# Keeping column-tiled matmul runs together, and moving score maxima ahead on VectorE, in a two-layer macaron transformer kernel

## The chip, the cores and the metric

The kernel runs on one core of one Trainium2 chip. The metric is the device time of one execution in microseconds (us), as a median of several runs. All intermediate results stay on the chip or in its HBM; there is one launch.

The engines are named as in the profile: PE is TensorE (PEld are its weight loads), DVE is VectorE, ACT is ScalarE, POOL is GpSimd, SP is the queue that issues most DMAs. Each engine works through its own list of instructions in the order that was fixed when the kernel was built, and waits on semaphores for what the others make.

## The reference, cut to what matters

The input is 16 sequences of 512 tokens of 128 features. Two layers are applied:

```
x = x + 0.5*ffn0(ln(x)); x = x + attn0(ln(x)); x = x + 0.5*ffn0(ln(x))     # layer 0
x = x + 0.5*ffn1(ln(x)); x = x + attn1(ln(x)); x = x + 0.5*ffn1(ln(x))     # layer 1
```

`ffn0` is a gated feed-forward net whose inputs and weights are rounded to a block-wise 4-bit format. `attn1` is a causal linear attention, and `ffn1` an attention over the batch, followed by a mixture of experts. The change is mostly about `attn0`, attention with clipped relative positions, 16 heads of 8 features:

```
score = einsum('bhqd,bhkd->bhqk', q, k) + einsum('bhqd,qkd->bhqk', q, pe_k)
attn  = softmax(score, axis=-1)
ctx   = einsum('bhqk,bhkd->bhqd', attn, v) + einsum('bhqk,qkd->bhqd', attn, pe_v)
```

Here `pe_k[q,k]` and `pe_v[q,k]` are rows of a table of 129 positions, picked by the distance `k-q` clipped to -64..64.

## The kernel before, in words

The kernel is written as Python generators that emit instructions. `interleave` decides in which order the generators advance, and so the program order. The framework then schedules: it plays the program forward on a model of the engines and, whenever an engine is free in that model, issues on it the ready instruction of the lowest priority number. By default that number is the place in program order. Two tools bend this. `tc.issue_after(ins)` forbids that the instructions of a block are issued before `ins` on the same engine. `tc.high_priority()` gives the instructions of a block a number ahead of everything of ordinary priority. What comes out is a fixed order for each engine; on the chip nothing is reordered by priority any more.

**Layer 0** works in 32 units, one for each sequence `b` and half of its queries (256 of 512). For each unit there are these streams:

- `Attn0.maxima` makes 32 score tiles of 128 keys by 512 (32 queries times 16 heads) in PSUM. A tile is made by `scores`: four matmuls with the keys (L263), and eight more with the position table (L267) if the tile lies in the band where the distance is not clipped. VectorE reduces each tile to its maxima (L341), and at the end of the unit the row maxima are written through DMA into the query operand `BD`, so that the second pass subtracts them.
- `Attn0.main` makes the same 32 tiles again. ScalarE takes the exponential of each into `PT` (L369), one of four SBUF tiles of 128 keys. After each eight tiles (`kt`, a block of 128 keys), a run of 16 matmuls multiplies `PT` with the values into two PSUM banks, `av`. Then, for each half `hb` of the unit whose last in-band key block this was, two runs multiply `PT` with the clipped position table `TV` into one PSUM bank, `rps`. ScalarE copies `rps` out (L404), it makes a trip through HBM, and `Attn0.fin` adds it to the rest (L423) and applies the output projection.
- `FFN.half` is the feed-forward net for half a sequence: transposes, matmuls of 352 columns, and a chain of rounding steps on VectorE and GpSimd. It runs once ahead (`head`) and once behind (`tail`) the attention.
- `Attn0.prep` and `prepV` make queries, keys and values for a sequence two ahead.

The score tiles of both passes share one PSUM pool of three banks (`pS`, the tile name is `sps`). A further two banks serve all the rest (`mps`).

The runs on `av` and `rps` are **column-tiled**: each matmul has only 32 output rows and uses a quarter of the array's columns (`tile_position=(0,cg*32)`), and four neighbours in the list, one for each quarter, work side by side. `Attn0.run` emits such a run: its first matmul (L272) at ordinary priority, the others (L274) behind it by `issue_after`. An `rps` run takes a pair of query blocks `bb`; for each it goes through the in-band key blocks `k` in rising order, with eight matmuls each. Over layer 0 there are 128 `av` runs of 16 matmuls and 128 `rps` runs of 28 matmuls on average. Each float32 matmul stands in the trace as two records, so such runs have 32 and on average 56 records.

**Layer 1** uses `Attn1.burst` (L853, L855) in the same way for its column-tiled runs: with the running state (`a_su`), with the masked products (`a_at`) and for the state's update (`a_kt`).

Of the kernel before, what the change touches and what calls it, by code (L numbers as in the profile page):

```python
# [13 lines left out]
ALU = mybir.AluOpType  # L14
AX = mybir.AxisListType
# [130 lines left out]
class Attn0:  # L146
# [123 lines left out]
    def run(a, mms):  # L270

        r=a.nc.tensor.matmul(*mms[0][0],**mms[0][1])  # L272
        with a.s.tc.issue_after(getattr(r,"ins",r)):
            for p,q in mms[1:]: a.nc.tensor.matmul(*p,**q)  # L274
    def prep(a, b, xb, wk, pM):
        s=a.s; nc=a.nc
# [55 lines left out]
    def maxima(a, b, half, wk, pS, pM):  # L332

        nc=a.nc; i=b%2
        u=(2*b+half)%3; BD=a.BD[u]; TQ=a.TQ[u]; KS=a.KS[b%2]; MD=a.MD[half]
        mx=wk.tile([128,4,16,8],F32,name="mx")
        for bb in range(8):
            for kt in range(4):
                ps=pS.tile([128,512],F32,name="sps")
                a.scores(ps,kt,half,bb,BD,TQ,KS)  # L340
                r=nc.vector.tensor_reduce(mx[:,kt,:,bb],ps.rearrange("p (i c) -> p i c",c=32),axis=AX.X,op=ALU.max,apply_transpose=True)  # L341
                a.last=r.ins if hasattr(r,"ins") else r
                yield
        a.last=None
        mk=wk.tile([128,2,8,8],F32,name="mk")
        for hh in range(2):
            nc.vector.tensor_reduce(mk[:,hh],mx.rearrange("p k (x s) b -> p s b x k",s=2)[:,hh],axis=AX.X,op=ALU.max)
        ps=pS.tile([128,512],F32,name="sps")
        nc.tensor.transpose(ps[:,:128],mk.rearrange("p s b x -> p (s b x)"),a.ident)
        mt=wk.tile([128,32],F32,name="mt"); mn=wk.tile([128,32],F16,name="mn")  # L350
        nc.vector.tensor_reduce(mt,ps[:,:128].rearrange("p (c q) -> p q c",c=4),axis=AX.X,op=ALU.max)
        nc.vector.tensor_scalar(mn,mt,-1.0,None,ALU.mult)
        for hh in range(2): nc.sync.dma_start(MD[hh*8:hh*8+8].rearrange("h (y j) -> y h j",j=4),mn[hh*64:hh*64+64].rearrange("p (h j) -> p h j",j=4))
        for j in range(4):
            nc.sync.dma_start(BD[28+32*j:29+32*j,:,j,:],MD.rearrange("(g j) q -> j g q",j=4)[j:j+1])
        yield

    def main(a, b, half, X, wk, big, pS, pA, pM):
        s=a.s; nc=a.nc; i=b%2
        u=(2*b+half)%3; BD=a.BD[u]; TQ=a.TQ[u]; KS=a.KS[b%2]; V=a.V[b%2]; RD=a.RD[half]; cr=a.cr[0]  # L360
        av=[pA.tile([128,512],F32,name=f"av{z}") for z in range(2)]
        RV=wk.tile([128,4,4,4,16],F32,name="RV")
        PT=[None]*4
        for kt in range(4):
            pt=big.tile([128,16,256],F32,name="PT"); PT[kt]=pt
            for bb in range(8):
                ps=pS.tile([128,512],F32,name="sps")
                a.scores(ps,kt,half,bb,BD,TQ,KS)
                nc.scalar.activation(pt[:,:,bb*32:bb*32+32].rearrange("p h (x j) -> p x h j",j=4),ps.rearrange("p (x h j) -> p x h j",x=8,j=4),AF.Exp)  # L369
                yield  # L370
            vs=a.vers(kt,half)
            mms=[]
            for z in range(4):
                for cg in range(4):
                    h=z*4+cg
                    o=av[z//2][cg*32:cg*32+32,(z%2)*256:(z%2)*256+256]
                    fs=(kt==0 and z%2==0)
                    mms.append(((o,V[:,2*kt-1+vs,h*9:h*9+32],pt[:,h,:]),dict(start=fs,stop=(kt==3),skip_group_check=True,tile_position=(0,cg*32))))
            a.run(mms)
            for _ in range(4): yield  # L380
            for hb in range(2):
                bl=range(hb*4,hb*4+4)
                ks=[k for k in range(4) if any(a.inband(k,half*8+x) for x in bl)]
                if max(ks)!=kt: continue
                rps=pA.tile([128,512],F32,name="rps")
                first=[True]*4
                mms=[]
                for bb in bl:
                    blk=half*8+bb
                    kk=[k for k in ks if a.inband(k,blk)]  # L390
                    for k in kk:
                        for x in range(8):
                            cg=x%4; col=(bb-hb*4)*128+(x//4)*64
                            v0=(blk*32-k*128+a.UO)//8
                            mms.append(((rps[cg*32:cg*32+32,col:col+64],a.TV[a.vers(k,half)][:,x,v0-8*a.vers(k,half):v0-8*a.vers(k,half)+4,:].rearrange("p v d -> p (v d)"),
                                PT[k][:,:,bb*32+4*x:bb*32+4*x+4]),
                                dict(start=first[cg],stop=(k==kk[-1]),skip_group_check=True,tile_position=(0,cg*32))))
                            first[cg]=False
                    if bb%2:
                        a.run(mms); mms=[]  # L400
                        yield
                        yield
                for c in range(4):
                    nc.scalar.copy(RV[:,:,c,:,hb*8:hb*8+8].rearrange("p j z a -> p a z j"),rps.rearrange("p (a z c j) -> p c a z j",a=8,z=4,j=4)[:,c])  # L404
                yield

        nc.sync.dma_start(RD[:,:4*8*1024].rearrange("x (r f) -> x r f",f=1024),RV)
        for c in range(4):
            src=bass.AP(tensor=RD.tensor,offset=RD.offset+c*64,ap=[[1024,8],[8*1024+256,16],[1,64]])
            nc.sync.dma_start(cr[c*32:c*32+8].rearrange("p (xj f) -> p xj f",f=64),src)  # L410
        cx=wk.tile([128,4,256],F32,name="cx")
        for zz in range(2):
            nc.scalar.copy(cx[:,2*zz:2*zz+2,:].rearrange("p z (b j x) -> p (z b) x j",j=4,x=8),av[zz].rearrange("p (y x j) -> p y x j",x=8,j=4))
        a.pend[b,half]=cx,cr
        yield
# [42 lines left out]
def layer0(tc, s, w, src, dst, nb=16):  # L458
# [3 lines left out]
    with ExitStack() as c:  # L462
# [44 lines left out]
        with tc.tile_pool(name="wp",bufs=1) as wp:  # L507
            for b in range(3): xload(b)
            F=FFN(s,w["L0_ffn_w_gate"],w["L0_ffn_w_up"],w["L0_ffn_w_down"],wp,pF)
            ffn2=lambda f,b: interleave((f(b,0),21,0,.8),(f(b,1),21,.2,1))  # L510
            ffn2(head,0)
            A=Attn0(s,wp,pS,*[w[P+n] for n in names])
            def run(g):
                for _ in g: pass
            run(prep(0)); run(prepV(0)); loads(0); run(mxs(0,0))
            FFN1.pre(s,wp,[pA.tile([128,512],F32,name=f"av{z}") for z in range(2)]+[pA.tile([128,512],F32,name="rps")],w)
        big=c.enter_context(tc.tile_pool(name="big",bufs=3))
        loads(1); ffn2(head,1); run(prep(1)); run(part(14)); ffn2(head,2)
        S=[(part(99999),33*2*nb,W['part'],2*nb+W['part'])]
        for b in range(nb):  # L520
# [262 lines left out]
class Attn1:  # L783
# [67 lines left out]
    def burst(a, mms):  # L851

        r=a.nc.tensor.matmul(*mms[0][0],**mms[0][1])  # L853
        with a.s.tc.issue_after(getattr(r,"ins",r)):
            for p,q in mms[1:]: a.nc.tensor.matmul(*p,**q)  # L855
    def main(a, t, bq, wk, pM, pP, pA):

# [181 lines left out]
```

## Time and profile before

| what | us |
|---|---|
| runs of the kernel | 3673.34, 3679.3, 3679.36 |
| median | 3679.3 |
| the profiled execution, its own time | 3669.38 |
| its span (first to last instruction) | 3667.4 |
| start-up: weights, first unit | 0 to about 180 of the span |
| layer 0 in steady work | about 180 to 2020 |
| layer 1: first `ffn1` | about 2020 to 2570 |
| layer 1: attention with parts of `ffn1` | about 2570 to 3420 |
| layer 1: end | about 3420 to 3668 |

The profile is one execution. Its own time is 2 us over the span, and 10 us under the median of the runs. Busy times of PE count matmuls that overlap only once, but a matmul counts as busy until its modelled end. To see what a matmul costs the ones behind it, this document takes the distance from its start to the start of the next. The mean granted clock of TensorE was 0.90 of full speed over the span.

### The profile page before, as it was taken

The numbers are of one execution on the slowest core, as the hardware profiler recorded it, in microseconds if no ns is written. First come the engines' busy times: TensorE is split into PE (matmuls) and PEld (weight loads), VectorE is DVE, ScalarE is ACT, GpSimd is POOL, SyncE is SP. The second block draws the span as 40 slices with busy tenths as digits, with TensorE's granted clock in tenths as the row PEclk, the third lists the DMA queues.
The fourth block names the chain that finished last, engine by engine and source line by source line (L and its number), as shares of the span: only waits on it lengthen the run. The fifth ranks groups of instructions, "written<-read, shape, count | busy, mean of one in ns | idle before, by whom it ended". The sixth has DMA issues, their size and how long they took to land. (4 is left out here: it accounts for less than half of the span.)

```text
span 3667.4 us, 95252 instructions
## 1 busy us (share of the span) xinstructions
PE 2895.4 (79%) x40077; PEld 2076.7 (57%) x40077; DVE 2453.7 (67%) x6508; ACT 1702.8 (46%) x3391; POOL 839.6 (23%) x789
## 2 busy tenths in 40 slices
PE   5579888898988989899988278882688888878570
PEld 3357666777767776677776144441465555555340
DVE  5568678777877788777764457774546656545357
ACT  3145445544554545545545155542455455445242
POOL 4122122222222222222101222222112121111226
PEclk8789999999999999999999588885899999999785
DMA  3232122322232122322210101104322222121301
GB/s 109 52 86 70 46 63 59 78 64 47 55 78 71 45 63 64 77 63 45 68 38 20 40 24 35 38 30 110 90 73 58 59 65 67 36 61 36 123 19 46
DMA packets 290159, 217.23 MB, mean 59 GB/s; under 512 B 77402, under 2 KB 257476, under 8 KB 289604
## 3 DMA queue, kind: packets, MB, share of 16 engines
q1 hardware_dynamic: 284468, 207.72, 21.5%
q8 instruction: 315, 5.16, 0.6%
q10 hardware_dynamic: 5264, 3.43, 0.4%
q14 instruction: 112, 0.92, 0.1%
HBM read 110.28 MB, written 100.78 MB: 58 GB/s over the span
## 5 line engine op out<-in xcount | busy, mean ns | idle before, releaser
L341 DVE TRANSPOSE_TENSOR_REDUCE mx<-sps 128x16 f32<-128x512 f32 x1024 | 706.0, 701 | 262.3 <-PE sps L267 138.6
L263 PE MATMUL sps<-a_BD,a_KS 128*128 128x128 f16 x8192 | 745.5, 222 | 156.2 <-DVE mx L341 96.2
L369 ACT ACTIVATE PT<-sps 128x512 f32<-128x512 f32 x1024 | 580.4, 598 | 554.0 <-PE sps L267 289.1
L263 PEld LDWEIGHTS <-a_KS 128*128 128x128 f16 x8192 | 540.3, 98 | 309.2 <-issue 257.7
L59 POOL TENSOR_TENSOR ln_rs<-ln_ve,negh 128x4 f32<-128x4 f32 (+1 forms) x192 | 175.3, 921 | 857.1 <-DVE ln_ve L58 778.3
L267 PE MATMUL sps<-a_TQ,a_ET 128*128 128x64 f16 x7168 | 370.2, 194 | 0.3 <-issue 0.3
L722 DVE SCALAR_TENSOR_TENSOR moe<-mps,oh,moe 128x128 f32<-128x128 f32 x896 | 289.8, 341 | 112.7 <-PE mps L720 99.7
L79 POOL TENSOR_TENSOR q_M<-q_y,q_M 128x704 f32<-128x704 f32 (+2 forms) x129 | 159.2, 1235 | 862.4 <-DVE q_y L78 650.7
L720 PE MATMUL mps<-f_W,T 128*128 128x512 f32 x512 | 302.9, 714 | 17.9 <-DVE moe L722 13.6
L267 PEld LDWEIGHTS <-a_ET 128*128 128x128 f16 x7168 | 309.8, 99 | 6.9 <-issue 6.5
L274 PE MATMUL av<-PT,a_V 128*32 128x256 f32 x3840 | 251.4, 386 | 0.0
L895 DVE TENSOR_TENSOR a_at<-pp,a_cm 128x1024 f32<-128x1024 f32 x128 | 154.4, 1215 | 71.7 <-PE pp L893 71.0
L274 PE MATMUL rps<-PT,a_TV 128*32 128x64 f32 x6912 | 199.5, 225 | 0.1
L893 PE MATMUL pp<-a_F 64*128 64x128 f32 x2048 | 165.1, 300 | 37.6 <-DVE a_at L895 29.9
L893 PEld LDWEIGHTS pp<-a_F 64*128 64x128 f32 x2048 | 139.3, 201 | 84.1 <-DVE a_at L895 36.0
L720 PEld LDWEIGHTS mps<-f_W,T 128*128 128x128 f32 x512 | 104.4, 227 | 118.5 <-issue 75.0
L274 PEld LDWEIGHTS av<-PT,a_V 128*32 128x32 f32 x3840 | 135.4, 111 | 55.8 <-issue 1.9
L274 PEld LDWEIGHTS rps<-PT,a_TV 128*32 128x32 f32 x6912 | 129.7, 110 | 50.1 <-issue 26.1
L875 ACT ACTIVATE a_F<-pp 128x1024 f32<-128x1024 f32 x128 | 127.0, 1027 | 45.5 <-PE pp L873 30.5
L62 ACT ACTIVATE xn<-xn,ln_mr,ln_rs 128x128 f32<-128x128 f32 x256 | 103.7, 483 | 87.8 <-DVE ln_mr L60 44.3
L139 PE MATMUL mps<-wdT,hT 128*128 128x128 f32 (+1 forms) x768 | 134.0, 313 | 7.6 <-ACT hT L136 7.3
L674 ACT COPY f_PT<-St 32x512 f32<-32x512 f32 x128 | 78.7, 615 | 105.4 <-DVE St L673 101.3
(342 smaller groups left out, 5338.3 us busy)
## 6 DMA issues: line engine op xcount, KB each, us to landing
QM<-a_HM SPq DMA_DIRECT2D x180, 128.0 KB
a_TQ<-QM SPq DMA_DIRECT2D x120, 192.0 KB
RD<-RV SPq DMA_DIRECT2D x32, 512.0 KB
a_KS<-KSd SPq DMA_DIRECT2D x128, 96.0 KB
a_QK<-a1d SPq DMA_DIRECT2D x128, 96.0 KB
xn<-X SPq DMA_DIRECT2D x32, 256.0 KB
a1d<-a_hi SPq DMA_DIRECT2D x64, 128.0 KB
a_BD<-QS SPq DMA_DIRECT2D x128, 58.0 KB
```

The lines of the kernel that those rows point to most:

```text
L59: nc.gpsimd.tensor_tensor(rs,ve,s.negh[:,:n],ALU.pow); yield
L79: nc.gpsimd.tensor_tensor(M[:P],y[:P],M[:P],ALU.subtract)
L139: nc.tensor.matmul(ps[:,384:512],hT[:P,c,:],f.wdT[:P,c,:],start=(c==0),stop=(c==2),skip_group_check=True)
L263: nc.tensor.matmul(o4[:,g],KS[:,sd,g*512+kt*128:g*512+(kt+1)*128],BD[:,g,:,b*32:b*32+32].rearrange("p h (x j) -> p x h j",j=4),start=(g==0 ...
L267: nc.tensor.matmul(out[:,x*64:x*64+64],a.ET[:,w0:w0+128],TQ[:,:,b*32+4*x:b*32+4*x+4],start=False,stop=(x==7),skip_group_check=True)
L274: for p,q in mms[1:]: a.nc.tensor.matmul(*p,**q)
L341: r=nc.vector.tensor_reduce(mx[:,kt,:,bb],ps.rearrange("p (i c) -> p i c",c=32),axis=AX.X,op=ALU.max,apply_transpose=True)
L369: nc.scalar.activation(pt[:,:,bb*32:bb*32+32].rearrange("p h (x j) -> p x h j",j=4),ps.rearrange("p (x h j) -> p x h j",x=8,j=4),AF.Exp)
L720: nc.tensor.matmul(ps,yT[:,j*128:(j+1)*128],a.W[:,e2*4:e2*4+4,:],start=True,stop=True)
L722: nc.vector.scalar_tensor_tensor(moe[:,j,:],ps[:,e*128:(e+1)*128],oh[:,j,e2*4+e:e2*4+e+1],moe[:,j,:],ALU.mult,ALU.add)
L893: nc.tensor.matmul(ps[:,hh,bs],f[hh*64:hh*64+64,1,bs],f[hh*64:hh*64+64,0,bs],start=True,stop=True)
L895: nc.vector.tensor_tensor(k,ps.rearrange("p h (b q) -> p (h b) q",b=4),a.cm.unsqueeze(1).to_broadcast([128,8,128]),ALU.mult)
```

## The change

It has three parts.

First, in `Attn0.run` and in `Attn1.burst`, all matmuls of a run but the first are traced under `tc.high_priority()`, as well as behind the first.

Second, the matmuls of an `rps` run are put in another order. For a pair of query blocks, the key blocks are now gone through from the last to the first, and inside a key block both query blocks follow each other, the later one first. So the first matmul of a run reads the part of `PT` that is made last. The number of matmuls, their shapes and their operands stay; only the places of the `start` and `stop` flags follow the new order.

Third, the reduction of each score tile to its maxima in `Attn0.maxima` is traced under `tc.high_priority()`.

```diff
     def run(a, mms):
         r=a.nc.tensor.matmul(*mms[0][0],**mms[0][1])
-        with a.s.tc.issue_after(getattr(r,"ins",r)):
+        with a.s.tc.issue_after(getattr(r,"ins",r)), a.s.tc.high_priority():
             for p,q in mms[1:]: a.nc.tensor.matmul(*p,**q)
...
                 a.scores(ps,kt,half,bb,BD,TQ,KS)
-                r=nc.vector.tensor_reduce(mx[:,kt,:,bb],ps.rearrange("p (i c) -> p i c",c=32),axis=AX.X,op=ALU.max,apply_transpose=True)
+                with a.s.tc.high_priority(): r=nc.vector.tensor_reduce(mx[:,kt,:,bb],ps.rearrange("p (i c) -> p i c",c=32),axis=AX.X,op=ALU.max,apply_transpose=True)
...
-                for bb in bl:
-                    blk=half*8+bb
-                    kk=[k for k in ks if a.inband(k,blk)]
-                    for k in kk:
+                for b0 in bl[::2]:
+                    ok=[(bb,k) for k in reversed(ks) for bb in (b0+1,b0) if a.inband(k,half*8+bb)]
+                    for n,(bb,k) in enumerate(ok):
+                        blk=half*8+bb
                         for x in range(8):
...
-                                dict(start=first[cg],stop=(k==kk[-1]),skip_group_check=True,tile_position=(0,cg*32))))
+                                dict(start=first[cg],stop=(k==min(q for p,q in ok if p==bb)),skip_group_check=True,tile_position=(0,cg*32))))
                             first[cg]=False
-                    if bb%2:
-                        a.run(mms); mms=[]
-                        yield
-                        yield
+                    a.run(mms); mms=[]
+                    yield
+                    yield
...
     def burst(a, mms):
         r=a.nc.tensor.matmul(*mms[0][0],**mms[0][1])
-        with a.s.tc.issue_after(getattr(r,"ins",r)):
+        with a.s.tc.issue_after(getattr(r,"ins",r)), a.s.tc.high_priority():
             for p,q in mms[1:]: a.nc.tensor.matmul(*p,**q)
```

## The prediction

> **What bounds the kernel now.** I read the page's busy times and its 40 slices first, then the busy times by stretch, the instructions of PE in order of time, PE's waits, and DVE's groups. The page:
>
> ```profile
> PE 2895.4 (79%) x40077; PEld 2076.7 (57%) x40077; DVE 2453.7 (67%) x6508; ACT 1702.8 (46%) x3391; POOL 839.6 (23%) x789
> ...
> PE   5579888898988989899988278882688888878570
> DVE  5568678777877788777764457774546656545357
> PEclk8789999999999999999999588885899999999785
> ```
>
> One digit is 92 us. Slices 3 to 22 are layer 0: PE at 8 to 9 tenths at nearly full clock, DVE at 7 to 8. The change's parts are nearly all there, and by stretch it is (PE, PEld, DVE, ACT, POOL busy, clock):
>
> ```profile
> 180.00:400.00 220.00, 190.43 (x3161) 145.39 (x3157) 165.54 (x348) 103.76 (x226) 48.66 (x44) 0.95 0.28 70
> 400.00:800.00 400.00, 353.23 (x6175) 279.94 (x6175) 302.32 (x691) 201.01 (x442) 93.17 (x89) 0.97 0.25 62
> 800.00:1200.00 400.00, 359.08 (x6088) 281.83 (x6088) 316.02 (x700) 200.57 (x438) 95.99 (x87) 0.97 0.27 66
> 1200.00:1600.00 400.00, 361.03 (x6164) 284.82 (x6164) 312.49 (x692) 200.81 (x437) 92.92 (x86) 0.97 0.24 57
> 1600.00:2020.00 420.00, 375.34 (x6977) 297.06 (x6973) 287.17 (x611) 217.99 (x466) 66.98 (x65) 0.97 0.20 50
> ```
>
> Over these 1840 us PE is busy 1639 (89%), DVE 1384 (75%), ACT 924 (50%). PE paces layer 0, with DVE close behind. PE in order of time, around 1016 and 1043 us:
>
> ```profile
> 1015.91 0.77 PE L274 MATMUL rps<-PT,a_TV 128*32 128x64 f32 x40
> 1016.61 0.40 PE L263 MATMUL sps<-a_BD,a_KS 128*128 128x128 f16 x4
> 1016.85 0.40 PE L267 MATMUL sps<-a_TQ,a_ET 128*128 128x64 f16 x8
> 1017.18 0.24 PE L272 MATMUL rps<-PT,a_TV 128*32 128x64 f32 x1
> ...
> 1043.77 0.43 PE L274 MATMUL rps<-PT,a_TV 128*32 128x64 f32 x13
> 1044.13 0.86 PE L125 MATMUL mps<-wguT,f_x 128*128 128x352 f32 x2
> 1044.92 0.26 PE L274 MATMUL rps<-PT,a_TV 128*32 128x64 f32 x4
> ```
>
> The first column is the start, the last the number of records. At 1044.13 a feed-forward matmul stands in the middle of an `rps` run, which goes on at 1044.92. The waits of PE, and DVE's group of maxima (busy, mean ns, idle before):
>
> ```profile
> PE sps L263 <- DVE mx L341: 88.1, 111, 10.2
> PE sps L263 <- ACT PT L369: 16.1, 45, 0.9
> L341 DVE TRANSPOSE_TENSOR_REDUCE mx<-sps 128x16 f32<-128x512 f32 x976 | 674.7, 702 | 245.5 <-PE sps L267 122.4 <-PE sps L263 119.7
> ```
>
> PE's longest wait is for a maxima reduction to free one of three score banks. DVE in turn idles 245.5 us before reductions, for PE.
>
> **Runs kept whole.** I sorted the matmuls of 180 to 2020 us by start and cut them into column-tiled stretches. There are 534: 406 hold `rps` records alone, 89 `av` alone (88 of these a whole run of 32), 39 both. So the `av` runs are whole already; it is the 128 `rps` runs that lie in 445 pieces. The price of a piece, by medians from its first start to the next full-width start: 8 records 252 ns, 16 363, 24 475, 32 587, 40 698. That is 111.5 ns for 8 records, plus 140 ns for each piece. Entering costs too: from an in-band tile's last L267 matmul to the next start is 28 ns where full-width work follows and 119 where a column-tiled piece does, 91 more (the fence shows it: 0.24 us at 1016.61, 0.33 at 1016.85). One piece too many costs 140+91 = 231 ns of PE.
>
> Whole runs leave at most 128+128 = 256 pieces, so 278 go: 278 x 0.231 = 64 us. Pieces that are no multiple of 8 records also cost almost a full group: 2 records take 231 ns, 8 take 252. The `rps`-only pieces sum to 156 us at their medians, to 146 by 140+13.94 ns a record: 10 more. Of the 26 us by which their real sum, 182, exceeds the medians (waits inside runs, such as a 5.3 us piece of 32 records), I count 6. Together 80 us of PE work.
>
> How much reaches the end? Taking PE work away shortens the stage only while PE is not waiting: 89%. In six of 31 stretches of 60 us DVE is busy for 49.5 us or more (51.06 in 780 to 840), and there I count nothing. 80 x 0.89 x 25/31 = 57 us; the ends are 0 (all turns into waits) and 80.
>
> The new order itself costs nothing in matmuls. Now the first one waits for the last exponential that the run reads, not an early one; what hides it is the other work that PE is given until then. Without that cover PE waits one exponential (L369, 0.598 us) in each of 128 runs, 77 us; but the runs are emitted after the `av` run of the same key block, which reads the whole `PT`, so I count nothing. Queued behind a run on PE are score tiles, for which ACT and DVE wait: 56 records cost 0.14+0.78 = 0.92 us, an `av` run 1.87 us already does so 128 times, and the banks hold up to three tiles; nothing. The single `rps` bank: PE waited 3.7 us for its copy (L404) in all; nothing.
>
> **Maxima first on DVE.** No instruction is added. I matched the 2048 score tiles to their readers, in both known orders: a reduction starts 0.81 us on average after its tile's last matmul (floor 0.037; exponentials 0.18), and before 474 of 1024 another DVE instruction was started in between. With priority these go behind. What can be gained is at most the 88 us. But three banks stay three, a reduction takes 0.70 us against 0.47 for an in-band tile, and PE will be back sooner: I take a sixth, 15 us. What is queued behind a reduction that waits is DVE's rounding chain, the normalizations and L423, and behind these POOL (L79 waits 585 us for L78 already) and the feed-forward matmuls. Their cover is the two or three sequences that `head` and `prep` run ahead; its loss is the slow rival. The other end of this term is there too, a loss of 120 us.
>
> **Layer 1.** From 2570 to 3420 us 104 bursts lie in 125 pieces: 21 x 0.231 = 5 us at most; as some neighbours join already and chains of waits lie between, I take 3, from 0 to 5.
>
> Sum: 57+15+3 = 75 us off the profiled execution's 3669.4, 3594. The median is 3679.3, 9.9 higher, so the forecast is **3604 us**.
>
> **The rivals.**
>
> *PE's gain turns into waits for PSUM.* DVE must still reduce 976 tiles at 0.70 us, and banks are held as long as now. Then the 80 us reappear as longer waits L263 <- L341: 3679. For it: that wait is the longest already, and DVE reaches 85% in its fullest 60 us. Against: PE waits only 201 of 1840 us in all, and DVE idles 456. The Trainium skill, in "TensorEngine Tiling (Array Packing)", section Performance Considerations, warns that tiling speeds up TensorE but not the emptying of PSUM, and that the copies out may become the limit. By that rule the time would stay at 3679; the 88.1 us wait bears it out in part. Chance 0.13.
>
> *Slower: DVE's list blocked by maxima.* A reduction is now put at the head of DVE's list as soon as the schedule's model has its tile ready. Where the chip's PE is later than the model, DVE stands, and everything behind it. Today 272 reductions wait, 242 us in all; the other 704 find their tile finished. If each of these waited one in-band tile (0.47 us), DVE would idle 331 us more. DVE's idle time that isn't before a reduction is 456-245 = 211 us and absorbs that much, so it decides from 0.30 us a reduction; at 0.47, 120 us land on the time: 3799, and PE's saving is hidden behind DVE. For it: 70% of the reductions have such slack to lose, and POOL and PE hang on the chain. Against: whole runs make PE's pace steadier. The Trainium skill, "TensorE: Matmul & The Clock Gate", section Architectural detail, says that VectorE's queue is strict first-in first-out; the 245.5 us idle before L341 agree. Chance 0.13.
>
> *The runs stay broken*, because the rest isn't ready when the first is issued, or the first is issued in pairs of idle moments as now. Only the 15 us remain, 3664. Against: the new order makes the first matmul the last to become ready. Chance 0.07.
>
> *Both parts in full*: 80 and 88 us and 5, 3506; at half of the 88, 3550. For it: every reduction that now waits behind others frees a bank earlier. Against: DVE would be at 83% over all of layer 0. Chance 0.12.
>
> **How the numbers follow.** The forecast, a gain of 35 to 115 us, has 0.55. This kernel's measurement can tell a change of about 0.2%, 7 us, from none. Faster: 0.55 + 0.12 + 0.06 of the broken runs + 0.04 of the first rival = 0.77. Same: 0.07 of the first rival, 0.01 of the broken runs = 0.08. Slower: 0.13 + 0.02 of the first rival = 0.15. The range goes from 3540, which takes in half of the mx waits on top of the full PE gain, to 3692, just past the first rival; left out are about 0.06 below and 0.13 above.
>
> **What would show it.** Right: column-tiled pieces of layer 0 fall from 534 to 256 or fewer, L272 is followed by all L274 of its run, PE's busy time from 180 us to the end of layer 0 falls by some 80 us, the wait L263 <- L341 falls below 88, and layer 1 keeps its length within 5 us. The delay of a reduction behind its tile falls from 0.81 us. Wrong: pieces fall and L263 <- L341 grows by as much (first rival); DVE's idle before L341 goes well over 245 us and POOL's wait for L78 grows (slow rival); pieces stay above 450 (broken runs). A longer layer 1 would be a shift that no term here holds.

## The result, and the profile after

The changed kernel takes 3633.0 us (median of 4 runs), against 3676.3 for the kernel before measured with it: a ratio of 0.9898, with a 95% interval of 0.987 to 0.9925. It is 43 us faster, where 75 were forecast. In the profiled executions, layer 0's attention, from the first to the last matmul that reads the table `a_TV`, shrank from 1838.7 to 1799.5 us, 39 us. What follows it went from 1648.9 to 1652.6 us.

The page of the changed kernel, the lines shown of before:

```profile
PE 2825.0 (78%) x40077; PEld 2032.3 (56%) x40077; DVE 2444.9 (67%) x6508; ACT 1693.8 (47%) x3391; POOL 838.9 (23%) x789
...
PE   5578989889898889888896388873788888878570
DVE  5568788777887788877773467774546655655356
PEclk8799999999999999999998599886899989989785
```

PE has 70 us less to do with the same 40077 matmuls, and DVE's and ACT's work is as before. The busy times by stretch (PE, PEld, DVE, ACT, POOL, clock), with the last stretch shorter by 40 us:

```profile
180.00:400.00 220.00, 187.40 (x3197) 144.66 (x3194) 166.52 (x354) 105.65 (x231) 48.88 (x44) 0.95 0.28 71
400.00:800.00 400.00, 354.63 (x6408) 280.14 (x6407) 309.27 (x704) 204.80 (x454) 96.00 (x91) 0.97 0.26 66
800.00:1200.00 400.00, 354.39 (x6220) 279.73 (x6221) 322.88 (x723) 203.30 (x448) 95.49 (x89) 0.97 0.25 63
1200.00:1600.00 400.00, 353.80 (x6412) 281.25 (x6411) 312.48 (x715) 204.79 (x457) 96.21 (x91) 0.98 0.25 63
1600.00:1980.00 380.00, 330.92 (x6338) 262.16 (x6326) 263.60 (x547) 195.01 (x416) 60.76 (x56) 0.97 0.20 48
```

Over these 1800 us PE is busy 1581 (before 1639 of 1840) and idle 219 (before 201). So PE's busy time fell by 58 us, and its idle time rose by 18.

PE in order of time, where two runs follow each other and then an `av` run:

```profile
1019.01 0.81 PE L125 MATMUL mps<-wguT,f_x 128*128 128x352 f32 x2
1019.75 0.24 PE L272 MATMUL rps<-PT,a_TV 128*32 128x64 f32 x1
...
1019.84 1.01 PE L274 MATMUL rps<-PT,a_TV 128*32 128x64 f32 x59
1020.78 0.40 PE L263 MATMUL sps<-a_BD,a_KS 128*128 128x128 f16 x4
...
1023.64 1.01 PE L274 MATMUL rps<-PT,a_TV 128*32 128x64 f32 x59
1024.47 0.38 PE L272 MATMUL av<-PT,a_V 128*32 128x256 f32 x1
```

From 1019.75 a run of 64 records goes through to 1020.78, in 1.03 us; the feed-forward matmuls stand before it, no longer in it. The waits of PE in layer 0 (total, times, longest):

```profile
PE sps L263 <- DVE mx L341: 59.1, 72, 9.0
PE sps L263 <- ACT PT L369: 35.5, 84, 2.6
PE mps L437 <- DVE a_V L321: 19.8, 12, 1.8
PE mps L440 <- ACT cn L438: 11.4, 9, 1.8
```

The third of these waits before, where L437 was L438 (no wait of the fourth kind was listed before):

```profile
PE mps L438 <- DVE a_V L321: 11.3, 10, 1.1
```

DVE's group of maxima in the changed kernel:

```profile
L341 DVE TRANSPOSE_TENSOR_REDUCE mx<-sps 128x16 f32<-128x512 f32 x976 | 671.1, 701 | 243.4 <-PE sps L263 136.6 <-PE sps L267 105.1
```

PE waits 29 us less for maxima and 19 us more for exponentials; DVE still idles 243 us for PE before reductions. Summed over all lines of this view, the waits before score matmuls (`sps`) fell from 138 to 125 us, and those before matmuls into the two `mps` banks rose from 48 to 76 us.

**PE's work and waits.** For the runs below, each matmul's distance to the next start was compared with the usual one for its kind and its successor's (the median of the kernels before and after, plus 15 ns). What is over counts as a wait of PE, the rest as work, over layer 0 as bounded above. The split depends on the count: with four column neighbours taken as one step, work falls by 66 us and waits rise by 27 from before to changed, in place of 77 and 38. Pieces are column-tiled stretches.

| kernel | layer 0, us | work | waits | pieces |
|---|---|---|---|---|
| before | 1838.7 | 1538.7 | 300.0 | 537 |
| changed | 1799.5 | 1461.6 | 337.9 | 241 |
| layer 0's runs and order alone (`runs_order`) | 1801.3 | 1462.2 | 339.1 | 241 |
| maxima's priority alone (`mx_only`) | 1852.4 | 1540.0 | 312.4 | 537 |
| layer 1's bursts alone (`burst_only`) | 1828.0 | 1537.5 | 290.5 | 537 |
| priority in the old order (`runs_oldorder`) | 1904.0 | 1483.6 | 420.4 | 335 |
| new order, no priority (`order_only`) | 1892.7 | 1513.1 | 379.6 | 430 |

Before, `mx_only` and `burst_only` run the same matmuls in the same order in layer 0; their 1828 to 1852 us show how far single profiled executions scatter. Their mean is 1839.7. The changed kernel and `runs_order` likewise have the same lists in layer 0; their mean is 1800.4.

### The profile page after: what moved, and what is told of

It reads as the page before. It is cut to its first block, busy times and chain, and to the rows that moved or that the text cites. A ratio compares the mean times of both kernels' runs of the same rounds, so it can differ in the third digit from the quotient of the medians.

```text
span 3632.2 us, 95259 instructions
## 1 busy us (share of the span) xinstructions
PE 2825.0 (78%) x40077; PEld 2032.3 (56%) x40077; DVE 2444.9 (67%) x6508; ACT 1693.8 (47%) x3391; POOL 838.9 (23%) x789
## 5 line engine op out<-in xcount | busy, mean ns | idle before, releaser
L341 DVE TRANSPOSE_TENSOR_REDUCE mx<-sps 128x16 f32<-128x512 f32 x1024 | 702.5, 701 | 261.7 <-PE sps L263 137.2
L263 PE MATMUL sps<-a_BD,a_KS 128*128 128x128 f16 x8192 | 736.4, 222 | 136.2 <-DVE mx L341 65.6
L369 ACT ACTIVATE PT<-sps 128x512 f32<-128x512 f32 x1024 | 576.4, 599 | 433.8 <-PE sps L267 238.1
L263 PEld LDWEIGHTS <-a_KS 128*128 128x128 f16 x8192 | 546.1, 98 | 296.4 <-issue 260.0
L267 PE MATMUL sps<-a_TQ,a_ET 128*128 128x64 f16 x7168 | 370.3, 195 | 0.0
L267 PEld LDWEIGHTS <-a_ET 128*128 128x128 f16 x7168 | 311.2, 99 | 2.3 <-issue 1.9
L274 PEld LDWEIGHTS av<-PT,a_V 128*32 128x32 f32 x3840 | 121.4, 111 | 68.7 <-issue 5.0
L274 PE MATMUL rps<-PT,a_TV 128*32 128x64 f32 x6912 | 134.5, 222 | 4.6 <-issue 4.4
L872 PE MATMUL pp<-a_QK,a_PK 128*128 128x512 f16 x256 | 82.7, 413 | 54.4 <-DMA a_QK<-a1d 26.6
```

The lines of the kernel that those rows point to most:

```text
L263: nc.tensor.matmul(o4[:,g],KS[:,sd,g*512+kt*128:g*512+(kt+1)*128],BD[:,g,:,b*32:b*32+32].rearrange("p h (x j) -> p x h j",j=4),start=(g==0 ...
L267: nc.tensor.matmul(out[:,x*64:x*64+64],a.ET[:,w0:w0+128],TQ[:,:,b*32+4*x:b*32+4*x+4],start=False,stop=(x==7),skip_group_check=True)
L341: with a.s.tc.high_priority(): r=nc.vector.tensor_reduce(mx[:,kt,:,bb],ps.rearrange("p (i c) -> p i c",c=32),axis=AX.X,op=ALU.max,apply_tr ...
```

## The experiments

All ratios are to the kernel before, run in the same session, with 95% intervals. The sessions differ: the median of before was 3653 in one and 3676 to 3685 in the others, so ratios are compared, not times.

**1. The parts one by one.** Layer 0's runs with priority and new order, without the maxima's priority and without layer 1's bursts:

```diff
 # the changed kernel, but
-        with a.s.tc.issue_after(...), a.s.tc.high_priority():     # in burst
+        with a.s.tc.issue_after(...):
-                with a.s.tc.high_priority(): r=nc.vector.tensor_reduce(mx...)
+                r=nc.vector.tensor_reduce(mx...)
```

> Layer 0's runs at the highest priority and in the new order; maxima and layer 1's bursts as before. Theory A (whole runs bring the gain, the maxima's priority brings nothing): 35 to 50 us faster than before, 3626 to 3641 at a before of 3676; 241 column-tiled pieces in layer 0 or nearly so; layer 0 shorter by about 39 us. Theory B (both parts bring some of it): 20 to 30 us faster. Theory C (the maxima's priority costs time that the runs earned): 55 to 80 us faster, 3596 to 3621.

Measured: 3635.8 us, 0.9878 (0.986 to 0.9897). That is theory A: the whole gain, with 241 pieces and layer 0 at 1801.3 us. On all engines, the lists of this kernel and of the changed one are the same, row for row, up to layer 1's first burst, so the maxima's priority moves nothing in the new order either.

The maxima's priority alone:

```diff
 # the kernel before, but
-                r=nc.vector.tensor_reduce(mx...)
+                with a.s.tc.high_priority(): r=nc.vector.tensor_reduce(mx...)
```

> Only the maxima at the highest priority. Theory A: within 7 us of before. Theory B: 10 to 25 us faster, with the wait of score matmuls for maxima down from 88 to about 59 us, as in the changed kernel. Theory C: 10 to 40 us slower. In all of them 534 or nearly so column-tiled pieces. If the delay of a reduction behind its tile stays near 0.8 us, the priority does not do on the chip what it is to do.

Measured: 1.0007 (0.9991 to 1.0024). The lists of instructions of PE, DVE, ACT, POOL and SP are the same as before, row for row (40077 on PE, 6508 on DVE). The edit does nothing. The order of the reductions was already what the scheduler gives them at the highest priority.

The priority in the old order, and the new order without priority:

```diff
 # runs_oldorder: the kernel before, but
-        with a.s.tc.issue_after(getattr(r,"ins",r)):              # in run
+        with a.s.tc.issue_after(getattr(r,"ins",r)), a.s.tc.high_priority():
 # order_only: the kernel before, but
-                for bb in bl: ... for k in kk:
+                for b0 in bl[::2]: ok=[(bb,k) for k in reversed(ks) for bb in (b0+1,b0) ...]
```

> Layer 0's runs at the highest priority, but in the old order (first matmul on the oldest exponentials). If the order is what makes a run ready as a whole: 280 to 400 pieces, and a gain of 10 to 30 us. If priority alone is enough: about 241 pieces and the gain of the kernel with both, within 8 us.

> The new order without any priority. If the order by itself makes runs ready as a whole, and so lets them run on: 300 to 450 pieces and 5 to 25 us faster. If the pieces come from ordinary priority alone (other work is ready and has a lower number): over 430 pieces and within 7 us of before.

Measured: `runs_oldorder` 1.0143 (1.0121 to 1.0165) with 335 pieces, `order_only` 1.012 (1.0101 to 1.0138) with 430. The pieces are near what was expected, the times are not: each half alone makes the kernel slower, by 53 and 44 us, and only both together make it faster. In the old order with priority, PE still breaks off in the middle of a run (PE in order of time in `runs_oldorder`):

```profile
1013.82 0.34 PE L274 MATMUL rps<-PT,a_TV 128*32 128x64 f32 x11
1014.09 0.40 PE L263 MATMUL sps<-a_BD,a_KS 128*128 128x128 f16 x4
1014.33 0.81 PE L125 MATMUL mps<-wguT,f_x 128*128 128x352 f32 x2
```

After 16 records of the run (11 of them in the first line), score and feed-forward matmuls follow, and the run goes on only at 1023.09, behind the next `av` run. In the old order the later matmuls of a run read later key blocks, whose exponentials come last, so priority has nothing ready to bring ahead. With both edits all 128 runs are whole (32 or 64 records each); with either alone they are not.

Layer 1's bursts alone:

```diff
 # the kernel before, but
-        with a.s.tc.issue_after(getattr(r,"ins",r)):              # in burst
+        with a.s.tc.issue_after(getattr(r,"ins",r)), a.s.tc.high_priority():
```

> Only layer 1's bursts at the highest priority; layer 0 as before. If the bursts bring what the prediction counted: 0 to 5 us faster and 104 pieces or fewer for 104 bursts in layer 1. If they cost the 4 us by which layer 1 got longer in the changed kernel's profile: 2 to 10 us slower. The changed kernel and the one with only layer 0's part differ by 0.2% in their ratios, which their intervals cannot tell apart.

Measured: 1.0006 (0.9988 to 1.0024). The pieces of layer 1's attention fell from 127 to 97, and no change of time is seen. The interval, 4 us faster to 9 us slower, holds both the 3 us that the prediction counted and the 4 us of loss, so neither is decided.

**2. Why each half alone is slower.** In `order_only`, PE's work fell by 26 us and its waits rose by 80. Ten stalls of PE of some 10 us stand out, one in every second unit, where the view names L58 on DVE (three such waits before, 9.1 us in all):

```profile
PE sps L263 <- DVE ln_ve L58: 98.2, 10, 10.9
```

One of them on the engines in order of time, first SP, then DVE, then PE:

```profile
796.97 1.31 SPq L486 DMA_DIRECT2D X<-x  x1
...
803.09 0.69 SPq L475 DMA_DIRECT2D x<-in_L_attn_x_dram  x1
```

```profile
809.03 1.07 DVE L55 BATCH_NORM_STATS2 ln_st<-x 128x6 f32<-128x128 f32 x5 [11.20 <-DMA x<-in_L_attn_x_dram]
```

```profile
811.09 0.58 PE L263 MATMUL sps<-a_BD,a_KS 128*128 128x128 f16 x4 [10.86 <-DVE ln_ve L58]
```

In brackets is the idle time before the instruction and what ended it. SP issues the load of the next sequence `x` at 803.09, behind other transfers; DVE has the normalization of `x` next in its list and stands 11.2 us, with reductions queued behind it; PE then stands 10.9 us for a score bank (the view names L58; the reduction L341 that frees the bank started at 810.36, right behind the normalization, and ended 0.05 us before PE went on). Such a stall costs more than its own length: from 811 to 815 us the granted clock is 0.50, against 1.00 from 797 to 800, and eight L267 matmuls take 0.44 us at 0.50 where they take 0.24 at 1.00 (medians over this trace). In all, DVE waits for `x` 117.5 us, against 43.4 before. SP's queue stands at the key load L315, ahead of the load of `x`, for PE; before, waits of this kind were 0.9 us in all:

```profile
SPq L315 <- PE sps L263: 273.6, 12, 26.6
```

Two edits were to take this away. The first traces the load earlier:

```diff
             nc.sync.dma_start(tok(dst,b)[:,2*h:2*h+2,:],X[b][:,2*h:2*h+2,:])
+            if h==1: xload(b+5)
```

> The new order without priority, with one more edit: the load of a sequence is traced as soon as the tail of the sequence whose buffer it takes is done, so one unit earlier than before. Theory A (the 44 us that the order alone cost are DVE waiting for a late load of x, 117 against 43 us, with PE behind it): 60 to 110 us faster than the order alone, 3610 to 3665, and the ten stalls of 9 to 16 us are gone. Theory B (the order itself costs, by another way): within 20 us of the order alone, 3705 to 3745, and PE's stalls move elsewhere.

> The kernel before with the same earlier load. DVE waits 43 us for x in the kernel before. Theory A: 15 to 43 us faster. If this wait is hidden: within 7 us.

> The changed kernel with the earlier load; DVE waits 45 us for x in it. Theory A: 15 to 45 us faster than the changed kernel, 3590 to 3620, so that the gain of the runs over the kernel before with the same edit stays 30 to 50 us. If the load is hidden here: within 8 us of 3633.

Measured: 1.0132 (1.0105 to 1.0158), 1.0011 (0.9992 to 1.0029) and 0.9929 (0.9906 to 0.9951). The theories are not told apart, for the edit does nothing: in all three pairs the lists of PE, DVE, ACT, POOL and SP are the same with it as without, row for row, and DVE waits 113.0 us for `x` in `order_xpre`. So these runs are repeats of three known kernels in another session. The loss of the order alone came out again (1.0132, before 1.012). The changed kernel's lists gained 26 us there (3626.8 against 3652.9), where they had gained 43: a ratio of 0.9929 against 0.9898, and 0.9878 for `runs_order`, so ratios of different sessions differ by up to half a per cent with the same layer 0. The second edit takes the load, and the store that frees its buffer, off SP's queue:

```diff
-            nc.sync.dma_start(t,tok(src,b))                       # load of x
+            nc.scalar.dma_start(t,tok(src,b))
-            nc.sync.dma_start(tok(dst,b)...,X[b]...)              # store of layer 0's result
+            nc.scalar.dma_start(tok(dst,b)...,X[b]...)
```

> The new order without priority; the load of x and the store of layer 0's result (which frees x's buffer) go through ACT's queue in place of SP's. In the order alone SP's queue stood 274 us in 12 waits of a key load (L315) for PE's score matmuls, with the store and the load of x queued behind it; DVE then waited 117 us for x, and PE for DVE. Theory A (this queue is the cause of the order's loss): DVE's wait for x falls below 40 us, the ten stalls of PE of 9 to 16 us go, and the time falls to 0.985 to 1.000 of before, from 1.012. Theory B (x is late for another reason, or the order costs in another way): 1.008 to 1.016 of before.

> Layer 0's runs at the highest priority in the old order (1.014 of before), with the load of x and the store that frees x's buffer on ACT's queue. In its trace a store at 1048.4, a load at 1052.2 and its landing at 1055.4 us kept DVE idle for 7.5 us and PE, behind DVE, for 6.1. Theory A (the late x costs these runs their gain, as it did with the order alone): 0.990 to 1.003 of before, DVE's wait for x from 66 to below 45 us. Theory B (PE's other waits, for the end of a unit's maxima and for broken runs, cost it): 1.008 to 1.02, or more where ACT now stands behind the two transfers, as in the changed kernel with this edit (1.032).

> The changed kernel with the same two transfers on ACT's queue. Its SP queue does not stand at L315; DVE waits 45 us for x. Theory A: DVE's wait falls and brings 10 to 40 us, 0.978 to 0.988 of before. Theory B: ACT's queue now stands behind the store, exponentials come later, and it is as the changed kernel or up to 20 us slower, 0.988 to 0.996.

Measured: `order_xact` 0.999 (0.9978 to 1.0001), from 1.012. `oldorder_xact` 1.0074 (1.0048 to 1.0099), from 1.0143. `after_xact` 1.032 (1.0301 to 1.0339), from 0.9898. DVE's waits for `x` and PE's behind L58, first DVE's in `order_only`, then both in `order_xact`:

```profile
DVE ln_st L55 <- DMA x<-in_L_attn_x_dram: 117.5, 11, 15.9
```

```profile
DVE ln_st L55 <- DMA x<-in_L_attn_x_dram: 65.0, 11, 8.9
PE sps L263 <- DVE ln_ve L58: 52.8, 10, 5.9
```

In `order_xact` PE's work stays at 1513.2 us with 428 pieces, and its waits fall from 379.6 to 326.7: with the load and the store off SP's queue, the loss of the order is gone. It does not go as far as expected: DVE's wait for `x` is 65 us and not under 40, and the ten stalls of PE are still there, at half their length. The edit also changes the lists of all engines, so what the queue alone costs is not separated from that.

In the old order with priority DVE's wait fell from 66 to 33 us, and half of the loss went; 1.0074 lies between the two theories. The other half lies in waits that this edit does not touch, among them 35 us for the reductions at a unit's end (L349 on L347, 33 us in `runs_oldorder`, 13 before). The clock has a part in it too: in layer 0 PE is busy at a granted clock of 0.50 for 87 us before, 141 in `runs_oldorder` and 108 in `oldorder_xact`; by the 0.24 and 0.44 us above, the 54 and 21 us more are an estimated 25 and 10 us of longer matmuls. How the rest divides stays open.

In the changed kernel the edit costs 4%, far beyond both theories: DVE's wait for `x` hardly moves (45 to 40 us), but PE's waits grow to 484.7 us. ACT stands there 95.6 us before L412 in eight waits, against none of this kind before, and the trace shows why. ACT in order of time, at one of them:

```profile
608.32 1.09 ACT L369 ACTIVATE PT<-sps 128x512 f32<-128x512 f32 x2
620.31 0.37 ACTq L486 DMA_DIRECT2D X<-x  x1
620.72 1.06 ACT L412 COPY cx<-av 128x512 f32<-128x512 f32 x1 [11.31 <-DMA a_TQ<-QM]
```

The moved store L486 stands in ACT's list ahead of L412, and ACT waits until it can issue it at 620.31; the transfer that the view names is not what held it. All eight waits look so. That is theory B's way, at a larger size. An edit that mends one schedule breaks another.

**3. Is the wait for `x` paid in the changed kernel?**

```diff
-        W=dict(part=0,V=(.6,.7),fin=(.45,.9),prep=(0,.7),tail=1.0,head=(-.1,1))
+        W=dict(part=0,V=(.6,.7),fin=(.45,.9),prep=(0,.7),tail=.8,head=(-.1,1))
```

> The changed kernel with the tail's feed-forward steps traced over 0.8 of a unit in place of 1.0, so that x's buffer is free some 11 us before the next load. If DVE's 45 us of waiting for x are paid at the end: 10 to 40 us faster than the changed kernel, 0.978 to 0.988 of before. If they are hidden, or the tail crowds DVE: 0.988 to 1.000.

Measured: 0.9906 (0.989 to 0.9922), and DVE's wait for `x` at 52.6 us. It is no better, and the wait was not removed, so what it costs in the changed kernel stays open. No kernel tried is faster than the changed one beyond the intervals; `runs_order` is its equal with two of the four edits in the diff.

## Why the prediction was right, point by point

**The runs, right.** It said 534 pieces fall to 256 or fewer: 241. It said 80 us of PE work: 77 (1538.7 to 1461.6), or 0.26 us for each of 296 pieces, where the steps gave 0.231 and the partial groups (by the other count of work and waits 66 us, 0.22 a piece). The price holds in between: `runs_oldorder` saves 55 us with 202 pieces less, `order_only` 26 with 107. A whole run of 64 records takes 1034 ns by the median, and 140+8x111.5 is 1032. One reading was loose: the fence's 0.24 us at 1016.61 is that of four L263 matmuls; that eight L267 matmuls with full-width work behind them take 0.24 us too is what makes the comparison with 0.33 hold.

**How much reaches the end, too high.** The step that took 89% and 25 of 31 stretches, and so 57 of 80 us, measured 39 in the profiles. By the table, half of the work saved came back as waits of PE, 38 of 77 us; by the busy and idle times of the stretches a third, 18 of 58. The two groups of equal layer 0 give the same difference (1839.7 to 1800.4). The step failed in holding that PE's idle share stays at what it was, and in looking for a limit in DVE's fullest stretches alone. The waits that grew are others: those of matmuls into `mps`, from 48 to 76 us, such as the one behind L321 (11.3 to 19.8) and the output projection's behind the copy L438 (none to 11.4). The other profiles of the same layer 0 agree: 41 and 47 in `burst_only` and `mx_only`, 73 in `runs_order`. That the work now gone had filled these moments is the likely reason, but it is argued. The first rival, that all of it returns as waits for PSUM, was right that a part returns, and wrong in the place: score matmuls wait less in all (138 to 125 us), less behind L341 by 29 us and more behind the exponentials by 19.

**Maxima first, wrong.** The term of 15 us is 0, by `mx_only`, whose lists are those of before, and by the changed kernel, whose layer 0 has the lists of `runs_order`. The delay of a reduction behind its tile is 0.78 us in the changed kernel, with another kind of DVE instruction started in between for 471 of 1024, hardly less than the 0.81 and 474 of before. I read this delay as a place in the queue that priority could better. It is no such place: in the lists these reductions have nothing ahead of them that priority moved. That the delay comes about because the chip's DVE runs behind the model is argued, not shown. For the same reason the slow rival could not come true by this edit, and the fall of L263 on L341 by 29 us came with the whole runs (52.7 us in `runs_order`).

**Layer 1, not decided.** 30 pieces went, by layer 0's price an estimated 7 us of PE work, and `burst_only` (1.0006, 0.9988 to 1.0024) excludes a gain of over 4 us. The 3 us of the prediction are too few to be told from none.

**The order at no cost, right only together.** It counted the new order at nothing and named as cover the other work that PE is given. That held with the priority: no wait of an `rps` matmul for L369 is listed in the changed kernel. Alone, the order costs 44 us, and the way is one that the prediction did not look at: it moves SP's queue, `x` comes late, and DVE's and PE's lists stand behind it. The changed kernel did not show the rival of broken runs; `runs_oldorder` shows its case, with 335 pieces left. There the price given for it, a gain of 15 us, was wrong in sign: 53 us slower.

The sum was 57+15+3 = 75; measured term by term it is 39 for the runs, 0 for the maxima, and for layer 1 too little to be seen. The ratio's 43 us and the profiles' 39 agree within the scatter of single profiles. That 43 lies within the forecast gain of 35 to 115 us is owed to the runs alone, and in part to luck: in the session of `after_xpre` the same lists gained 26.

## What to carry to other kernels

A switch between full-width and column-tiled matmuls has a price that can be read from starts (here 0.22 to 0.26 us a piece), so count the pieces of each run; to keep a run whole, its first matmul must be the one that becomes ready last, and the rest must go ahead of all else, both at once. Where lists are made on a model, compare the lists before costing a priority or running an experiment: an edit that leaves them the same is worth nothing, however long the delay on the chip; here that was so for the maxima's priority and for the earlier load. Expect a part of a saving to come back as waits (here a third to a half), in places other than the longest wait of before. And look at the queues that an edit moves indirectly: here a late load, shifted by a new order on another engine, outweighed the saving, and moving its store to ACT's list made ACT stand behind it in another schedule.

## What the runs showed of the hardware that was not expected

A column-tiled run that follows another has no price of its own: an `rps` run of 64 records and an `av` run of 32 take 2.76 us together, where apart they take 1.03 and 1.87, 2.90 us; the 0.14 us are the leaving part of the price. And the same layer-0 lists took 1828.0, 1838.7 and 1852.4 us in three profiled executions in different sessions, and those of `order_only` 1892.7 and, as `order_xpre`, 1866.5 us, so a difference of 20 us between two single profiles says nothing.
